# The end of a ranking: rows from a root, stores first, two groups in turns

## The chip, the cores and the metric

The kernel runs on one core of a Trainium2 chip. A core has five engines with queues of their own: TensorE (PE, with its weight load PEld), VectorE (DVE), ScalarE (ACT), GpSimd (POOL) and SyncE (SP), which here only issues transfers. Sixteen DMA engines move the data. The metric is device time of one execution in microseconds; smaller is better.

## The reference, cut to what matters

The program is a network of four layers on a tensor of 4 x 64 channels x 128 x 128, 12 ms long. The change lies in layer 1, in the first of its two parts. There each of 256 images (128 rows of 128 values each) gets a 128 x 128 matrix of squared distances between its rows, and every entry is replaced by a weight that depends only on its rank among all 16,384 entries of that image:

```python
def score_to_weight(score):
    n = shp[-1] * shp[-2]
    flat = score.reshape(-1, n)
    tau = jnp.argsort(-flat, axis=-1)
    ranks = (jnp.argsort(tau, axis=-1) + 1).astype(score.dtype) / n
    weights = -jnp.log(ranks).reshape(shp)
    return weights / jnp.sum(weights, axis=-1, keepdims=True)
```

The matrix is symmetric, so only the 8128 pairs above its diagonal are sorted. A pair's two entries take two ranks that follow each other. Where two distances are equal, the stable order of `argsort` decides, and that needs the places (row and column) of the pairs concerned.

## The kernel before, in words

**The ranking (`l1_ranks`).** The 256 images are two groups `g` of 128, one image to a partition. `keys[g]` is a tile of 128 x 8192 f32 (8128 pairs and padding). A merging network sorts it, and stores for each of its 91 stages which pairs turned (`sort_stage`, DVE, ACT and POOL). `number` marks equal neighbours in `ranks[g]`, an int16 tile of 128 x 8192. Then the stages are run backwards over the ranks (`back_stage`, DVE and ACT), so that each rank comes to stand at the place of its pair. The sorting and the way back take from 2004 to 5131 us of the profile.

**The end of the ranking (`finish`, L1548 to L1634),** called for group 0 and then for group 1. The steps that matter:

- *cast:* ACT copies the ranks to f32 into the group's own `keys` tile, free by then (L1551).
- *candidates:* DVE takes the eight largest of each of 32 segments of 256, with their indices (L1555, L1556). Marked ranks are above the others, so these are the pairs with equals.
- *spread:* DVE takes the marks off with an AND (L1558); ACT writes rank + 129 and rank + 130 beside each other as int16 into the tile `spare`, in two activations (L1561); SP stores the result to the memory tensor `pk[g]`, one transfer for each of the 127 rows of the matrix above the diagonal, since they shrink from 127 entries to one (L1565).
- *list:* the 64 largest candidates are found by eight rounds of MAX8 and MATCH_REPLACE8 (L1580, L1582), and their fields taken apart (L1586 to L1589): the pair's number `f`, whether it is equal to the next (`more`) and `tied`.
- *row:* `f` is compared with the 128 row ends, a constant tile loaded from memory, and the hits are summed (L1596, L1601); the column follows from the row (L1603 to L1607).
- *order among equals:* positions are compared all with all, 128 x 128 a partition, into the group's `keys` tile, and summed (L1620, L1625).
- *turn:* column, row and lack of each listed pair are copied to `both`, transposed on PE and copied to `ties` by ACT (L1631 to L1634).

`spare` is one tile for both groups. `cand`, `at`, `both` and the other small tiles have two buffers. Last, `m` collects a flag that says whether equals were too many for the list (L1656 to L1662); all engines load it, and an `If` (L1833) runs a slow full sort when it is set, which it is not here. Behind the `If` stands `l1_blocks`, which loads constants and then the stored ranks.

**What sets the order.** Sorting and the way back are in an order written out by hand. The end of the ranking is not: a scheduler orders the instructions of each engine at build time by their dependencies, so pieces of group 1 stand between those of group 0 already. Within an engine, instructions go in that order; SP issues its transfers one after the other.

Of the kernel before, what the change touches and what calls it, by code (L numbers as in the profile page):

```python
# [10 lines left out]
F32 = mybir.dt.float32  # L11
I32 = mybir.dt.int32
U32 = mybir.dt.uint32
I8, I16 = mybir.dt.int8, mybir.dt.int16
U8 = mybir.dt.uint8
BF16 = mybir.dt.bfloat16
AF = mybir.ActivationFunctionType
ALU = mybir.AluOpType
AX = mybir.AxisListType
# [3 lines left out]
P = 128  # L23
B, H, W, C = 4, 64, 128, 128
# [1025 lines left out]

def l1_constants():

    return {"l1c_rowend": np.asarray(ROW0[1:] + [1 << 20], np.float32),
            "l1c_diag": np.ascontiguousarray(np.diag(np.arange(1, W + 1)).reshape(W * W), np.int32)}


def rnn_inputs(env, x, xn, gram):
# [349 lines left out]
ROW0 = [n * (2 * W - 1 - n) // 2 for n in range(W)]  # L1407

SEG, TIES = 256, 64
# [43 lines left out]
def l1_ranks(env, dscr, keys, pk, masks, ties, tables):  # L1453
# [5 lines left out]
    nc, tc = env.nc, env.tc  # L1459
# [3 lines left out]
    with ExitStack() as ctx:  # L1463
        kp = ctx.enter_context(tc.tile_pool(name="sk", bufs=1))
        mp = ctx.enter_context(tc.tile_pool(name="sm", bufs=3))
        sb = ctx.enter_context(tc.tile_pool(name="sb", bufs=2))
        ranks = [kp.tile([P, NSORT], I16, name="rank%d" % g) for g in range(2)]
        bad = kp.tile([P, 2, 34], F32, name="bad")
        rowend = kp.tile([P, W], F32, name="rowend")
        nc.sync.dma_start(rowend, tables["rowend"].partition_broadcast(P))  # L1470
        segs = kp.tile([P, NSORT // SEG, 8], I32, name="segs")
        nc.gpsimd.iota(segs, [[SEG, NSORT // SEG], [0, 8]], base=0, channel_multiplier=0)
        place = kp.tile([P, 2 * TIES], I32, name="place")
# [5 lines left out]
        base = kp.tile([P, 2], F32, name="base")  # L1479
# [64 lines left out]

            nc.vector.tensor_scalar(bad[:, g, 0:1], v[:, 0:1], 1e-30, None, ALU.is_le)

        def finish(g, ta, tb):

            r = ranks[g]
            rf = ta  # L1550
            nc.scalar.copy(rf, r)  # L1551
            cand = sb.tile([P, NSORT // SEG, 8], F32, name="cand")
            at = sb.tile([P, NSORT // SEG, 8], U32, name="at")
            for s in range(NSORT // SEG):
                nc.vector.max(cand[:, s, :], rf[:, s * SEG : (s + 1) * SEG])  # L1555
                nc.vector.max_index(at[:, s, :], cand[:, s, :], rf[:, s * SEG : (s + 1) * SEG])  # L1556

            nc.vector.tensor_single_scalar(r, r, 16382, ALU.bitwise_and)  # L1558
            pt = tb.bitcast(I16).rearrange("q (f s) -> q f s", s=2)
            for s in range(2):  # L1560
                nc.scalar.activation(pt[:, :, s], r, AF.Identity, bias=base[:, s : s + 1])  # L1561
            pv = pk[g][0 : P * W * W, :].rearrange("(t f) o -> t (f o)", t=P)
            pi = tb.bitcast(I32)
            for n in range(W - 1):
                nc.sync.dma_start(  # L1565
                    pv[:, n * W + n + 1 : (n + 1) * W], pi[:, ROW0[n] : ROW0[n] + W - 1 - n]
                )

            nc.vector.tensor_scalar(bad[:, g, 1:33], cand[:, :, 7], 16383.5, None, ALU.is_gt)
            ci = sb.tile([P, NSORT // SEG, 8], I32, name="ci")  # L1570
            cp = sb.tile([P, NSORT // SEG, 8], I32, name="cp")
            nc.vector.tensor_tensor(ci, at.bitcast(I32), segs, ALU.add)
            nc.vector.tensor_copy(cp, cand)
            nc.vector.tensor_single_scalar(cp, cp, 13, ALU.logical_shift_left)
            nc.vector.tensor_tensor(cp, cp, ci, ALU.bitwise_or)
            nc.vector.tensor_single_scalar(cp, cp, 1 << 29, ALU.bitwise_or)
            cf = cp.rearrange("q s e -> q (s e)").bitcast(F32)
            top = sb.tile([P, TIES], F32, name="top")
            for t in range(0, TIES, 8):
                nc.vector.max(top[:, t : t + 8], cf)  # L1580
                if t + 8 < TIES:
                    nc.vector.match_replace(cf, top[:, t : t + 8], cf, 0.0)  # L1582

            def field(name, shift, mask):
                a = sb.tile([P, TIES], I32, name="fi")
                nc.vector.tensor_single_scalar(a, top.bitcast(I32), shift, ALU.logical_shift_right)  # L1586
                nc.vector.tensor_single_scalar(a, a, mask, ALU.bitwise_and)
                f = sb.tile([P, TIES], F32, name=name)
                nc.vector.tensor_copy(f, a)  # L1589
                return f  # L1590

            f, more, tied = field("f", 0, 8191), field("more", 13, 1), field("tied", 27, 1)
            nc.vector.tensor_copy(bad[:, g, 33:34], tied[:, TIES - 1 : TIES])

            cmp = ta.rearrange("q (i n) -> q i n", n=W)
            nc.vector.tensor_tensor(  # L1596
                cmp, f.unsqueeze(2).to_broadcast([P, TIES, W]), rowend.unsqueeze(1).to_broadcast([P, TIES, W]),
                ALU.is_ge,
            )
            row = sb.tile([P, TIES], F32, name="row")  # L1600
            nc.vector.tensor_reduce(row, cmp, AX.X, ALU.add)  # L1601
            col = sb.tile([P, TIES], F32, name="col")
            nc.vector.tensor_scalar(col, row, -0.5, W - 0.5, ALU.mult, ALU.add)  # L1603
            nc.vector.tensor_mul(col, col, row)
            nc.vector.tensor_sub(col, f, col)
            nc.vector.tensor_add(col, col, row)
            nc.vector.tensor_scalar(col, col, 1.0, None, ALU.add)  # L1607
            pos = sb.tile([P, 2, TIES], F32, name="pos")
            nc.vector.scalar_tensor_tensor(pos[:, 0, :], row, float(W), col, ALU.mult, ALU.add)
            nc.vector.scalar_tensor_tensor(pos[:, 1, :], col, float(W), row, ALU.mult, ALU.add)  # L1610

            run = sb.tile([P, TIES], F32, name="run")
            nc.vector.tensor_scalar(more, more, -1.0, 1.0, ALU.mult, ALU.add)
            nc.vector.tensor_tensor_scan(run, one, more, 0.0, ALU.mult, ALU.add)
            for s in range(2):
                nc.vector.scalar_tensor_tensor(pos[:, s, :], run, -32768.0, pos[:, s, :], ALU.mult, ALU.add)
            pf = pos.rearrange("q s i -> q (s i)")
            n2 = 2 * TIES
            before = ta.bitcast(I16).rearrange("q (i j) -> q i j", j=n2)
            nc.vector.tensor_tensor(  # L1620
                before, pf.unsqueeze(1).to_broadcast([P, n2, n2]), pf.unsqueeze(2).to_broadcast([P, n2, n2]), ALU.is_lt
            )
            rk = sb.tile([P, 2, TIES], F32, name="rk")
            rv = rk.rearrange("q s i -> q (s i)")
            nc.vector.tensor_reduce(rv, before, AX.X, ALU.add)  # L1625
            nc.vector.tensor_add(rv, rv, listed)
            nc.vector.tensor_mul(rk, rk, tied.unsqueeze(1).to_broadcast([P, 2, TIES]))
            for k, pair in enumerate(((col, row), (row, col), (rk[:, 0], rk[:, 1]))):
                both = sb.tile([P, 2, TIES], F32, name="both")
                for h in range(2):  # L1630
                    nc.vector.tensor_copy(both[:, h], pair[h])  # L1631
                pt = psum.tile([P, P], F32, name="pt")
                nc.tensor.transpose(pt, both.rearrange("q s i -> q (s i)"), env.ident)  # L1633
                nc.scalar.copy(ties[:, k, g * P : g * P + P], pt)  # L1634
# [4 lines left out]
        with tc.tile_pool(name="low", bufs=2, space=PSUM) as lows, tc.tile_pool(  # L1639
            name="diff", bufs=4  # L1640
# [4 lines left out]
        spare = ctx.enter_context(tc.tile_pool(name="spare", bufs=1)).tile([P, NSORT], F32, name="spare")  # L1645
        for g in range(2):
            number(g, keys[g], spare)
        with tc.manual_schedule(engines={E.Activation, E.DVE}):
            for i in range(ns):
                for g in range(2):  # L1650
                    back_stage(g, ns - 1 - i)
        psum = ctx.enter_context(tc.tile_pool(name="sp", bufs=1, space=PSUM))
        finish(0, keys[0], spare)
        finish(1, keys[1], spare)
        m = kp.tile([P, 1], F32, name="m")
        nc.vector.tensor_reduce(m, bad, AX.XY, ALU.max)  # L1656
        pm = psum.tile([1, P], F32, name="pm")
# [1728 lines left out]
def metaformer(tc, a, out, cst):  # L3386

    with ExitStack() as ctx:
        env = Env(ctx, tc)
        nc = tc.nc  # L3390
        dp = ctx.enter_context(tc.tile_pool(name="dram", bufs=1, space=DRAM))
        state = [dp.tile([NI, W, C], F32, name="state%d" % i) for i in range(5)]
        tokens = dp.tile([NI, W, C], F32, name="tokens")
        dist = dp.tile([NI, W * W], F32, name="dist")

        pk = [dp.tile([P * W * W, 1], I32, name="pk%d" % g) for g in range(2)]
        masks = [dp.tile([P, sum(NSORT // (2 * p) * (p - k if k < p else p) for p, k in merge_network(NSORT))], I8,
                         name="masks%d" % g) for g in range(2)]
        def part(prefix):
            return {k[len(prefix) :]: v for k, v in a.items() if k.startswith(prefix)}  # L3400

        x = a["x"].rearrange("b h w c -> (b h) w c")
        f0, f2 = part("L0_ffn_"), part("L2_ffn_")

        def diagonals():
# [5 lines left out]
        l0_conv(env, x, state[0], tokens, part("L0_conv_"), cst, diagonals)  # L3411
        rnn_ffn(env, state[0], state[1], f0["W"], f0["VT"], f0["gamma"], f0["beta"])
        l1_layer(
            env, state[1], state[2], dist, pk, masks, part("L1_conv_"), part("L1_ffn_"), {"rowend": cst["l1c_rowend"]}
        )
        l2_conv(env, state[2], state[3], part("L2_conv_"))
        rnn_ffn(env, state[3], state[4], f2["W"], f2["VT"], f2["gamma"], f2["beta"])
# [37 lines left out]
```

## Time and profile before

| | us |
|---|---|
| median of 3 runs | 11948.84 |
| lowest, highest of them | 11933.74, 11949.3 |
| the profiled execution | 11937.16 |
| its span | 11935.4 |
| distances and all before, 0 to 2003.7 | 2003.7 |
| sorting and way back, to 5123.4 | 3119.7 |
| end of the ranking, 5123.4 to 5325.3 | 201.9 |
| layer 1's blocks, to 6300 | 974.7 |
| the rest | 5635 |

Over the whole span DVE is busy 84%, ACT 63%, PE 61%, POOL 52%. These shares mix stages with different limits: in the end of the ranking DVE is busy 184.2 of 201.9 us, ACT 53.0, PE 3.1 and POOL 0.2. A line of the profile's order of time gives start, length, engine, line of the kernel, operation, the tiles written and read, shapes and count, and in brackets how long the engine had been idle and what ended that. A name such as SPq is the engine's queue, in which transfers are issued.

### The profile page before, as it was taken

What the parts mean: (1) busy time and instruction counts of PE and PEld (TensorE: products, weight loads), DVE (VectorE), ACT (ScalarE), POOL (GpSimd) and SP (SyncE); (2) the same over time, 40 slices, a digit from 0 to 9 for tenths busy, and PEclk for the clock granted to TensorE, in tenths of its full rate; (3) what the DMA queues carried; (4) which work ended last, traced back from release to release, by engine and by line L of the source; (5) the groups of instructions that cost most, each with busy time, mean ns of one, the idle gap of its engine ahead of it and who ended that gap; (6) DMA issues with size and microseconds to landing.
All of it is one profiled execution on the core that took longest, in us unless ns stands there. A gap on an engine that the chain in (4) does not pass through costs nothing. (4 is left out here: it accounts for less than half of the span.)

```text
span 11935.4 us, 113939 instructions
## 1 busy us (share of the span) xinstructions
PE 7337.1 (61%) x33966; PEld 4454.9 (37%) x33966; DVE 10014.6 (84%) x16358; ACT 7522.4 (63%) x10863; POOL 6182.3 (52%) x5276
## 2 busy tenths in 40 slices
PE   7887796000000000009998899989999999998665
PEld 5665564000000000008886344444444444446443
DVE  7566637999999999988996899999999999996444
ACT  4255534888867777633332778777878787875332
POOL 1000016999970000002332899998999999994222
PEclk8876798555555555559999899999999999999887
DMA  4223245111111111121111343433333334333434
GB/s 139 89 43 100 63 149 140 56 57 58 58 56 54 55 54 56 49 49 42 47 45 35 129 143 140 144 135 137 135 140 139 143 138 143 139 133 117 169 131 152
DMA packets 632396, 1193.48 MB, mean 100 GB/s; under 512 B 216556, under 2 KB 433998, under 8 KB 552398
## 3 DMA queue, kind: packets, MB, share of 16 engines
q1 hardware_dynamic: 587550, 1043.02, 26.1%
q0 software_dynamic: 34656, 140.92, 3.6%
q8 instruction: 274, 4.49, 0.2%
q10 hardware_dynamic: 9552, 2.08, 0.1%
q14 instruction: 364, 2.98, 0.1%
HBM read 950.89 MB, written 251.71 MB: 101 GB/s over the span
## 5 line engine op out<-in xcount | busy, mean ns | idle before, releaser
L2717 POOL TENSOR_TENSOR gs<-hist,cc 128x512 f32<-128x512 f32 x2048 | 2576.5, 1266 | 378.9 <-DVE hist L2712 217.1
L2712 DVE TENSOR_TENSOR_SCAN hist<-da,state,bs 128x512 f32<-128x512 f32 x1984 | 2523.9, 1272 | 0.0
L2726 PE MATMUL py<-gs,ident 128*128 128x512 f32 x4096 | 2246.0, 631 | 5.1 <-DVE y L2602 3.7
L1633 PE MATMUL pt<-ident,both 128*128 128x128 f32 x6 | 2.7, 447 | 3258.0 <-DVE both L1631 3258.0
L2683 ACT ACTIVATE da<-dt,am 128x512 f32<-128x512 f32 x2048 | 1414.8, 715 | 325.6 <-DVE hist L2712 323.0
L2704 DVE TENSOR_TENSOR bs<-dx,bs 128x512 f32<-128x512 f32 x2048 | 1393.8, 681 | 187.7 <-PE bs L2690 143.0
L1509 POOL TENSOR_TENSOR diff<-key 128x2048 f32<-128x2048 f32 (+11 forms) x364 | 1383.8, 3861 | 86.8 <-DVE key L1514 75.2
L1633 PEld LDWEIGHTS pt<-ident,both 128*128 128x128 f32 x6 | 1.1, 183 | 3259.5 <-issue 3259.5
L2726 PEld LDWEIGHTS py<-gs,ident 128*128 128x128 f32 x4096 | 739.3, 197 | 902.5 <-issue 441.2
L1884 POOL IOTA row<- 72x1 int32 x1 | 0.1, 136 | 1800.7 <-ACTq L1833 1800.7
L2690 PE MATMUL bs<-bt,pick 96*128 96x512 bf16 x2048 | 807.3, 394 | 140.3 <-DVE hist L2712 137.3
L1531 ACT COPY keep<-rank 128x1536 int16<-128x1536 int16 (+11 forms) x364 | 612.8, 1686 | 437.9 <-DVE rank L1533 389.0
L1507 ACT COPY low<-key 128x2048 f32<-128x2048 f32 (+11 forms) x364 | 626.7, 1722 | 285.1 <-DVE key L1514 276.4
L1532 DVE COPY_PREDICATED rank<-back,rank 128x1536 int16<-128x1536 uint8 (+11 forms) x364 | 781.8, 2148 | 16.7 <-ACT keep L1531 16.7
L1533 DVE COPY_PREDICATED rank<-back,keep 128x1536 int16<-128x1536 uint8 (+11 forms) x364 | 778.0, 2137 | 12.5
L1514 DVE TENSOR_TENSOR key<-low,key 128x2048 f32<-128x2048 f32 (+11 forms) x364 | 744.5, 2045 | 12.4
L1513 DVE TENSOR_TENSOR key<-low,key 128x2048 f32<-128x2048 f32 (+11 forms) x364 | 749.2, 2058 | 6.5 <-DMA key<-dist 6.2
L1510 ACT ACTIVATE turned<-diff 128x2048 int8<-128x2048 f32 (+11 forms) x364 | 600.0, 1697 | 36.4 <-DMA key<-dist 27.6
L1522 ACT ACTIVATE back<-turned 128x3072 uint8<-128x3072 int8 (+12 forms) x182 | 582.3, 3200 | 0.0
L2183 PE MATMUL pe<-ew,xg 128*128 128x128 f32 x4096 | 504.4, 277 | 0.0
L1031 POOL DMA_DIRECT2D state<-zz x16 | 18.6, 1161 | 909.7 <-DVE zz L1021 854.5
L2183 PEld LDWEIGHTS pe<-ew,xg 128*128 128x128 f32 x4096 | 488.2, 193 | 3.9
(826 smaller groups left out, 18502.8 us busy)
## 6 DMA issues: line engine op xcount, KB each, us to landing
cc<-cd SPq DMA_DIRECT2D x512, 1024.0 KB
xt<-state SPq DMA_DIRECT2D x64, 1024.0 KB
xo<-state SPq DMA_DIRECT2D x128, 256.0 KB
state<-xo POOLq DMA_DIRECT2D x128, 256.0 KB, 2.8
xl<-in_L_ffn_weight SPq DMA_DIRECT2D x32, 1024.0 KB
tk<-in_x SPq DMA_DIRECT2D x32, 512.0 KB
tokens<-tt POOLq DMA_DIRECT2D x32, 512.0 KB, 5.2
tk<-tokens SPq DMA_DIRECT2D x8, 2048.0 KB
```

The costliest lines, as they stand in the source:

```text
L1509: nc.gpsimd.tensor_sub(d, lo[part], hi[part])
L1513: nc.vector.tensor_tensor(lo[part], c, hi[part], ALU.min)
L1514: nc.vector.tensor_tensor(hi[part], c, hi[part], ALU.max)
L1532: nc.vector.copy_predicated(l, t, h)
L1533: nc.vector.copy_predicated(h, t, kv)
L2183: T.matmul(w["pe"][:, j, :], w["xg"][:, q, j, :], ew[:, q, :], start=False, stop=(j == 3 and q == E - 1))
L2683: nc.scalar.activation(da, x_["dt%d" % b], AF.Exp, scale=am[:, s : s + 1])
L2690: nc.tensor.matmul(bs, pick[:, s, :], x_["bt%d" % b], start=True, stop=True)
L2704: nc.vector.tensor_mul(db, x_["dx%d" % b], db)
L2712: nc.vector.tensor_tensor_scan(h, live.pop(("da", t)), live.pop(("db", t)), 0.0 if first else state[b][:, s : s + 1], ALU.mult, ALU.add,)
L2717: nc.gpsimd.tensor_tensor(gs, h, live.pop(("cc", t)), ALU.mult)
L2726: nc.tensor.matmul(x_["py%d" % b], env.ident, live.pop(("gs", t)), start=(s == 0), stop=(s == S - 1))
```

## The change

`finish` is cut into `spread`, `candidates`, `equals`, `compare` and `lacking`, and these are called for the two groups in turns. Group 1's ranks are spread into `keys[1]` in place of `spare`, and group 1's comparison of all with all goes into `keys[0]`. The AND and the stores are put ahead of the candidates. The row of a listed pair is no longer found with 128 comparisons: it is the rounded value of a root, (255 - sqrt(255^2 - 8 f)) / 2, the root made by Ln and Exp on ACT, and is then put right by one down or up by looking whether `f` lies before the row's start or behind its end. The constant of row ends is gone, with its load.

```diff
-        rowend = kp.tile([P, W], F32, name="rowend")
-        nc.sync.dma_start(rowend, tables["rowend"].partition_broadcast(P))
...
-        def finish(g, ta, tb):
+        def spread(g, pt):
             r = ranks[g]
-            rf = ta
-            nc.scalar.copy(rf, r)
...
+            nc.vector.tensor_single_scalar(r, r, 16382, ALU.bitwise_and)
+            halves = pt.bitcast(I16).rearrange("q (f s) -> q f s", s=2)
+            for s in range(2):
+                nc.scalar.activation(halves[:, :, s], r, AF.Identity, bias=base[:, s : s + 1])
+            pv = pk[g][0 : P * W * W, :].rearrange("(t f) o -> t (f o)", t=P)
+            pi = pt.bitcast(I32)
+            for n in range(W - 1):
+                nc.sync.dma_start(
+                    pv[:, n * W + n + 1 : (n + 1) * W], pi[:, ROW0[n] : ROW0[n] + W - 1 - n]
+                )
+
+        def candidates(g, rf):
             cand = sb.tile([P, NSORT // SEG, 8], F32, name="cand")
...
+            return cand, at
+
+        def equals(g, cand, at):
...
-            cmp = ta.rearrange("q (i n) -> q i n", n=W)
-            nc.vector.tensor_tensor(
-                cmp, f.unsqueeze(2).to_broadcast([P, TIES, W]), rowend.unsqueeze(1).to_broadcast([P, TIES, W]),
-                ALU.is_ge,
-            )
+            x = sb.tile([P, TIES], F32, name="x")
+            nc.vector.tensor_scalar(x, f, -8.0, float((2 * W - 1) ** 2), ALU.mult, ALU.add)
+            nc.vector.tensor_scalar(x, x, 1.0, None, ALU.max)
+            nc.scalar.activation(x, x, AF.Ln)
+            nc.scalar.activation(x, x, AF.Exp, scale=0.5)
+            ri = sb.tile([P, TIES], I32, name="ri")
+            nc.vector.tensor_scalar(ri, x, -0.5, W - 0.5, ALU.mult, ALU.add)
             row = sb.tile([P, TIES], F32, name="row")
-            nc.vector.tensor_reduce(row, cmp, AX.X, ALU.add)
+            nc.vector.tensor_copy(row, ri)
+            gap = sb.tile([P, TIES], F32, name="gap")
+
+            def start():
+                nc.vector.tensor_scalar(gap, row, -0.5, W - 0.5, ALU.mult, ALU.add)
+                nc.vector.tensor_mul(gap, gap, row)
+                nc.vector.tensor_sub(gap, f, gap)
+
+            start()
+            nc.vector.scalar_tensor_tensor(row, gap, 0.0, row, ALU.is_lt, ALU.subtract)
+            nc.vector.tensor_scalar(row, row, -1.0, None, ALU.mult)
+            start()
+            nc.vector.tensor_add(x, gap, row)
+            nc.vector.scalar_tensor_tensor(row, x, W - 1.0, row, ALU.is_ge, ALU.add)
+            start()
             col = sb.tile([P, TIES], F32, name="col")
-            nc.vector.tensor_scalar(col, row, -0.5, W - 0.5, ALU.mult, ALU.add)
-            nc.vector.tensor_mul(col, col, row)
-            nc.vector.tensor_sub(col, f, col)
-            nc.vector.tensor_add(col, col, row)
-            nc.vector.tensor_scalar(col, col, 1.0, None, ALU.add)
+            nc.vector.scalar_tensor_tensor(col, gap, 1.0, row, ALU.add, ALU.add)
...
-        finish(0, keys[0], spare)
-        finish(1, keys[1], spare)
+        for g in range(2):
+            nc.scalar.copy(keys[g], ranks[g])
+        spread(0, spare)
+        found = [candidates(0, keys[0])]
+        found.append(candidates(1, keys[1]))
+        last = [equals(0, *found[0])]
+        before = [compare(last[0][3], keys[0])]
+        spread(1, keys[1])
+        last.append(equals(1, *found[1]))
+        lacking(0, *last[0][:3], before[0])
+        before.append(compare(last[1][3], keys[0]))
+        lacking(1, *last[1][:3], before[1])
```

`compare` holds the comparison of all with all (L1620 before), and `lacking` its sum and the turn to `ties` (L1625 to L1634).

More of the change, by code (lines that the diff above doesn't have):

```diff
@@ L1051, in l1_constants @@
 def l1_constants():
-    return {"l1c_rowend": np.asarray(ROW0[1:] + [1 << 20], np.float32),
-            "l1c_diag": np.ascontiguousarray(np.diag(np.arange(1, W + 1)).reshape(W * W), np.int32)}
+    return {"l1c_diag": np.ascontiguousarray(np.diag(np.arange(1, W + 1)).reshape(W * W), np.int32)}
 def rnn_inputs(env, x, xn, gram):
@@ L1556, in finish @@
                 nc.vector.max_index(at[:, s, :], cand[:, s, :], rf[:, s * SEG : (s + 1) * SEG])
[L1558 to L1566, printed above, removed]
-                )
+            return cand, at
+        def equals(g, cand, at):
             nc.vector.tensor_scalar(bad[:, g, 1:33], cand[:, :, 7], 16383.5, None, ALU.is_gt)
@@ L1593, in finish @@
             nc.vector.tensor_copy(bad[:, g, 33:34], tied[:, TIES - 1 : TIES])
-            cmp = ta.rearrange("q (i n) -> q i n", n=W)
-            nc.vector.tensor_tensor(
-                cmp, f.unsqueeze(2).to_broadcast([P, TIES, W]), rowend.unsqueeze(1).to_broadcast([P, TIES, W]),
-                ALU.is_ge,
-            )
-            row = sb.tile([P, TIES], F32, name="row")
-            nc.vector.tensor_reduce(row, cmp, AX.X, ALU.add)
-            col = sb.tile([P, TIES], F32, name="col")
-            nc.vector.tensor_scalar(col, row, -0.5, W - 0.5, ALU.mult, ALU.add)
-            nc.vector.tensor_mul(col, col, row)
-            nc.vector.tensor_sub(col, f, col)
-            nc.vector.tensor_add(col, col, row)
-            nc.vector.tensor_scalar(col, col, 1.0, None, ALU.add)
+            x = sb.tile([P, TIES], F32, name="x")
[5 more added lines that the diff above has]
+            nc.vector.tensor_scalar(ri, x, -0.5, W - 0.5, ALU.mult, ALU.add)
+            row = sb.tile([P, TIES], F32, name="row")
+            nc.vector.tensor_copy(row, ri)
[11 more added lines that the diff above has]
+            start()
+            col = sb.tile([P, TIES], F32, name="col")
+            nc.vector.scalar_tensor_tensor(col, gap, 1.0, row, ALU.add, ALU.add)
             pos = sb.tile([P, 2, TIES], F32, name="pos")
@@ L1616, in finish, with compare @@
                 nc.vector.scalar_tensor_tensor(pos[:, s, :], run, -32768.0, pos[:, s, :], ALU.mult, ALU.add)
+            return row, col, tied, pos
+        n2 = 2 * TIES
+        def compare(pos, room):
             pf = pos.rearrange("q s i -> q (s i)")
-            n2 = 2 * TIES
-            before = ta.bitcast(I16).rearrange("q (i j) -> q i j", j=n2)
+            before = room.bitcast(I16).rearrange("q (i j) -> q i j", j=n2)
             nc.vector.tensor_tensor(
@@ L1622, in finish, with lacking @@
             )
+            return before
+        def lacking(g, row, col, tied, before):
             rk = sb.tile([P, 2, TIES], F32, name="rk")
@@ L3413, in metaformer @@
         l1_layer(
-            env, state[1], state[2], dist, pk, masks, part("L1_conv_"), part("L1_ffn_"), {"rowend": cst["l1c_rowend"]}
+            env, state[1], state[2], dist, pk, masks, part("L1_conv_"), part("L1_ffn_"), {}
         )
```

## The prediction, made before the changed kernel ran

> **What bounds the kernel now.** I began with the busy time of each engine in stretches of the span, to find the changed part and see who works there. Columns: stretch, its length, then busy time and instruction count of PE, PE's weight load, DVE, ACT, POOL.
>
> ```profile
> 5123.40:5175.10 51.70, 0.00 (x0) 0.00 (x0) 51.63 (x170) 32.74 (x5) 0.00 (x0) 0.50 0.00 0
> 5175.10:5235.50 60.40, 1.34 (x3) 0.55 (x3) 60.40 (x67) 0.80 (x3) 0.00 (x0) 0.50 0.31 69
> 5235.50:5262.00 26.50, 0.00 (x0) 0.00 (x0) 25.84 (x64) 18.70 (x2) 0.00 (x0) 0.50 0.01 0
> 5262.00:5324.10 62.10, 1.72 (x4) 0.63 (x4) 46.30 (x27) 0.80 (x3) 0.14 (x1) 0.50 0.31 68
> ```
>
> The end of the ranking takes 201 us of 11935.4. DVE is full for three stretches, but in the last it works 46.3 of 62.1 us: something else ends the stage. The transfers run in the second and fourth stretch only (31% of the DMA engines), so I asked for the stores of the ranks and for the order of time around them (start, length, engine, line, operation, count).
>
> ```profile
> L1565 SPq DMA_DIRECT2D pk<-spare x254: 319/430/1406, 5175.1 to 5323.3; - x127
> ```
> ```profile
> 5123.42 7.01 ACT L1551 CAST key<-rank 128x8192 f32<-128x8192 int16 x1
> ...
> 5131.15 7.02 ACT L1551 CAST key<-rank 128x8192 f32<-128x8192 int16 x1 [0.72 <-DVE rank L1533]
> ...
> 5154.06 2.28 DVE L1558 TENSOR_SCALAR rank<-rank 128x8192 int16<-128x8192 int16 x1
> ...
> 5156.37 18.69 ACT L1561 ACTIVATE spare<-rank,base 128x8192 int16<-128x8192 int16 x2 [18.20 <-DVE rank L1558]
> ...
> 5171.62 8.68 DVE L1596 TENSOR_TENSOR key<-f,rowend 128x8192 f32<-128x8192 f32 x1
> ```
> ```profile
> 5192.59 17.22 DVE L1620 TENSOR_TENSOR key<-pos 128x16384 int16<-128x16384 f32 x1
> ...
> 5243.28 18.70 ACT L1561 ACTIVATE spare<-rank,base 128x8192 int16<-128x8192 int16 x2 [13.30 <-DVE rank L1558]
> ...
> 5309.17 0.27 ACT L1634 COPY ties<-pt 128x128 f32<-128x128 f32 x1 [17.93 <-PE pt L1633]
> ```
> ```profile
> 5325.28 0.17 DVE L1868 MEMSET rw<- 128x128 f32 x1 [16.73 <-SPq L1833]
> 5325.37 0.39 SPq L1847 DMA_DIRECT2D enc<-in_L_conv_enc_w  x1
> ```
>
> SP issues 127 stores a group. Group 0's run from 5175.1 to 5235.5 (60.4 us, 0.476 each), group 1's from 5262.0 to 5323.7 (61.7 us); between them SP stands 26.5 us, because both groups go through the one tile `spare`, which ACT fills for group 1 only at 5243.3 to 5262.0. DVE and ACT are done at 5309.4; then DVE waits 16.7 us for SP at the `If` (L1833). So **SP's stores set the end of this stage**, and everything after it starts at 5325.3.
>
> **What the Trainium skill says.** *Perfetto Trace Analysis*, What "DMA-bound" means: a kernel can be bound by the issuing sequencer, its track solid with DMA slices, which are descriptor generation and not data movement. The trace agrees: issues back to back at 0.476 us with DMA engines 31% busy. *ScalarE: Activation LUTs*, Table sets: Ln and Exp share one set, so that the pair needs one load. Here Ln and Exp of L1950 and L1951 run at 5348.73 and 5348.97 with no load ahead since the distances, and in the changed kernel's order no load stands ahead of the new pair. *ScalarE*, What ACT_TABLE_LOAD costs: an activation takes 186 ns + 0.833 ns an element, an estimate of 0.24 us for 64; the trace has 0.26 us for 128x64 (L2126).
>
> **The change part by part.** The built order of instructions gives each engine's sequence; I walk it with the trace's durations.
>
> *Ranks first (ACT, SP).* The AND on group 0's ranks goes ahead of the 32 pairs of maximum and index search (5131.01 to 5154.06, 23.05 us), so it runs from 5131.0 to 5133.2, off ACT's path. ACT does both casts first (the second ends at 5138.2), then the two spreading activations: 5138.2 + 18.7 = 5156.9. SP starts there and not at 5175.1: **18.2 us earlier**. Group 0's stores end at 5156.95 + 60.4 = 5217.4.
>
> *Second buffer.* Group 1's spread goes into `keys[1]`, free once group 1's candidates have been read. DVE: 5133.2 + 2 x 23.05 = 5179.3, three small operations (0.1 + 0.33 + 0.2), AND 2.2: 5182.2. ACT: 5182.25 + 18.7 = 5200.9, which is 16.5 us before SP needs it. So SP's gap of **26.5 us goes**; the wait of this activation on all the earlier stores goes as well, since it has no DMA wait in the new order. SP: 5217.4 + 61.7 = 5279.1, last issue and branch 0.4: 5279.5. Before it branched at 5324.1: 44.6 earlier. If the cover of 16.5 us failed, each us beyond it would be paid.
>
> *Root in place of the table (DVE).* Out: per group one 8.68 us compare (L1596) and one 8.68 us sum (L1601), issued 8.6 apart: 4 x 8.6 = 34.4 us. In: 13 more operations of 128x64 a group (18 in place of 5); the trace gives 0.10 to 0.12 us each where another group's stand between, 0.2 us alone. 26 x 0.12 = 3.1 us. On ACT, Ln and Exp twice; they are queued behind group 1's spread, which the new order makes ACT finish at 5200.9, then two of 0.26 in a chain: DVE can go on at 5201.5.
>
> *DVE's walk.* At 5182.2: rest of the key building of both groups 2.0 us, 16 MAX8 at 0.33 and 14 replace pairs at 0.39 = 10.7, fields, scan and the two operations ahead of Ln 3.1: 5198.0. Wait for ACT to 5201.5 (3.5 us). Then 39 small operations at 0.12 to 0.13: 5206.5. Then compare 17.14 (issue to issue), four small 0.6, sum 17.12, a few small 0.4, compare 17.14, 0.2, sum 17.12: 5276.2. A check by difference: before, DVE took 5131.0 to 5308.5 = 177.5; less 34.4, plus 3.1, plus 3.5, less about 3 us of latency gaps that group 1's lone chain had (5243 to 5253 and 5271 to 5273) and that turns now fill: 146.7, so 5277.7.
>
> *Tail.* Both `both` buffers are full, so four transposes with their ACT copies (0.45 + 0.27 + semaphores, about 0.78 each) and the last operations of group 1 come after the last sum: ACT ends near 5280.0. Before, one stood there. Then the branch: ACT's came 0.4 us after its copy (5309.8) and its first semaphore event after it at 5313.1. These 3.3 us were hidden under SP's stores; **now they are late next**: 5280.0 + 0.4 + 3.3 = 5283.7, while SP is through at 5279.5 + 1.3 = 5280.8. SP's first load after the `If` waits on ACT and DVE, so it goes at about 5283.7 and not at 5325.37: **gain 41.7 us**.
>
> *At nothing.* The `rowend` load leaves SP's queue at 2044.4, where SP is idle till its next issue at 2047.5 for lack of masks; if it were not hidden, 0.33 us gained. Three more 256-byte tiles move addresses only. PE now transposes `m` first; `m` is ready at about 5198, before any `both`.
>
> Sum: 11937.16 (profiled execution; its span 11935.4) - 41.7 = 11895.5. The median shown is 11948.84 over 11933.74 to 11949.3; from it, 11907.1. I take the middle, **11902**.
>
> **Bounds on what the trace does not show.** The branch's 3.3 us exposed: from nothing (SP last, gain 44.6) to 3.3. Small operations in turns: 0.10 to 0.2 us over 39 + 26, so DVE from 1.5 us less to 5 us more. Ln and Exp: no load in the order; were there one it is 1.28 us by the row at 5349.19. Store rate beside other DVE work: 0.476 to 0.486 in both stretches, so 0 to 2.5 us. Together a gain of 34 to 45 us.
>
> **Rivals.**
> 1. *Only the earlier start is won.* Something still holds group 1's spread until group 0's stores have landed, and SP's gap stays 20 us or more: 5217.4 + 26.5 + 61.7 leaves 18.2 us, 11919 to 11931. For: SP still runs both groups in order. Against: the tiles differ, and the activation waits on DVE and ACT alone. 4%.
> 2. *DVE becomes the clear bound.* ACT's spread slows or the root's chain runs at 0.3 us a step: DVE ends 8 to 14 us later, gain 27 to 34, 11908 to 11918. For: after the change DVE and SP end within 3 us of each other, so any slip shows in full. Against: the steps have the other group's between them. 12%.
> 3. *SP stays last* with the branches hidden: gain 44.6, 11892 to 11904. 20%.
> 4. *Slower.* The stores now overlap DVE's candidate search and ACT's spread; if this stretched each from 0.476 us, SP, which has 254 in one line, would take the whole loss. It decides at 44.6 / 254 = 0.176 us more, 0.65 a store; at 0.75 the time would be 11968. For: a single store took up to 1.4 us. Against: the second stretch, with ACT idle, and the first have the same 0.43 us median. 3%.
> 5. *It does not do what it says*: a compiler that keeps one order for both groups, so nothing is gained, 11940. The built order excludes most of it. 1%.
>
> **How the numbers follow.** The forecast has 60%: gain 36 to 44, 11890 to 11914 over the two baselines. With rivals 2 and 3 the gain runs from 27 to 45; taken against a baseline that itself moves over 15 us, eight in ten lie in 11887 to 11918. About 0.2% (24 us) is what a measurement of this kernel can tell from no change. Faster by more: the forecast, rivals 2 and 3 (92%), less some 3% for a baseline drawn low: 0.89. Within: rivals 1 and 5 and that 3%: 0.08. Slower: 0.03.
>
> **What would show it.** Stores of group 0 begin near 5157 and SP has no gap near the 128th; ACT's third spread begins near 5182 with a wait on DVE; the two 8.68 us rows are gone; DVE waits about 3.5 us for ACT's Exp; the first load after the `If` comes near 5284, released by ACT's or DVE's branch and not by SP's. A gap in SP, a table load, or stores over 0.5 us apart would show me wrong.

## The result, and the profile after

| | before | after |
|---|---|---|
| median of 5 runs, us | 11948.84 | 11889.27 |
| lowest to highest, us | 11932.91 to 11949.59 | 11866.29 to 11901.57 |
| profiled execution, its span, us | 11937.16, 11935.4 | 11866.29, 11864.5 |

The ratio is 0.9954, 95% interval 0.9941 to 0.9968: faster by 0.46%, some 55 us, and by more than 0.2% over the whole interval. The prediction said 11902 in a range of 11887 to 11918.

Times within the profiles do not compare directly, since the stages ahead of the change, which it leaves alone, ended 4.7 us later in this execution. From here on *the stage* runs from the end of the way back on DVE (the AND's start after the change, the first search for candidates before it) to the first load behind the `If`. Before, it ran from 5131.0 to 5325.4, **194.4 us**; after, from 5135.7 to 5288.2, **152.5 us**. That is 41.9 us less, where the prediction had 41.7.

The busy time of the engines in stretches of the span, after the change, cut at the first store, between the groups and at the branch (stretch, length, then PE, PE's weight load, DVE, ACT, POOL, each with its count, then TensorE's granted clock, the busy share of the DMA engines and GB/s):

```profile
5135.70:5161.50 25.80, 0.00 (x0) 0.00 (x0) 25.80 (x100) 25.59 (x3) 0.00 (x0) 0.50 0.00 0
5161.50:5222.10 60.60, 0.37 (x1) 0.08 (x1) 57.59 (x221) 19.22 (x6) 0.00 (x0) 0.50 0.31 69
5222.10:5283.00 60.90, 1.95 (x5) 0.81 (x5) 60.24 (x23) 1.06 (x4) 0.00 (x0) 0.50 0.31 69
5283.00:5288.20 5.20, 0.88 (x2) 0.29 (x2) 0.00 (x0) 0.53 (x2) 0.01 (x1) 0.50 0.04 6
```

Of before's four stretches the third, 26.5 us with no store, is gone, and the first, ahead of the stores, is 25.8 us from the stage's start where it was 44.1. DVE is now busy through both stretches of stores but for one wait of 2.9 us, where it stood for 16 us in the second. A new stretch has come at the end: 5.2 us in which nothing but a few transposes and copies of 0.3 us runs.

The stores, from the view of their line after the change (shortest, median, longest issue in ns, first and last start):

```profile
L1554 SPq DMA_DIRECT2D pk<-spare x127: 319/430/558, 5161.5 to 5221.6; - x127
L1554 SPq DMA_DIRECT2D pk<-key x127: 320/430/485, 5222.2 to 5282.1; - x127
```

And in order of time (start, length, engine, line, operation; in brackets the idle time ahead and its end):

```profile
5142.79 18.66 ACT L1550 ACTIVATE spare<-rank,base 128x8192 int16<-128x8192 int16 x2
...
5187.01 18.69 ACT L1550 ACTIVATE key<-rank,base 128x8192 int16<-128x8192 int16 x2 [25.56 <-DVE rank L1547]
...
5206.12 0.34 DVE L1602 TENSOR_SCALAR ri<-x 128x64 int32<-128x64 f32 x2 [2.94 <-ACT x L1600]
...
5211.08 17.22 DVE L1639 TENSOR_TENSOR key<-pos 128x16384 int16<-128x16384 f32 x1
...
5263.73 17.21 DVE L1648 TENSOR_REDUCE rk<-key 128x128 f32<-128x16384 int16 x1
```
```profile
5284.27 0.27 ACT L1657 COPY ties<-pt 128x128 f32<-128x128 f32 x1 [0.57 <-PE pt L1656]
5288.19 0.40 SPq L1880 DMA_DIRECT2D enc<-in_L_conv_enc_w  x1
5288.19 0.14 POOL L1917 IOTA row<- 72x1 int32 x1 [1770.89 <-ACTq L1866]
5288.27 0.17 DVE L1901 MEMSET rw<- 128x128 f32 x1 [5.36 <-ACTq L1866]
```

Group 1's spread now waits for DVE's AND alone and is done 16 us ahead of the first store that needs it. Behind the `If`, DVE waits for ACT's queue (ACTq), where it had waited 16.7 us for SP's. The view of the `If`'s line says what lies between ACT's last copy and there:

```profile
L1866 SPq COMPARE_BRANCH  x1: 50/50/50, 5283.0 to 5283.0; - x1
...
L1866 ACTq COMPARE_BRANCH  x1: 45/45/45, 5284.9 to 5284.9; - x1
...
L1866 ACTq EVENT_SEMAPHORE  x1: 17/17/17, 5288.1 to 5288.1; - x1
```

SP is at its branch at 5283.0. ACT branches at 5284.9 and shows its next event at 5288.1: 3.2 us that stand on the path now. Before, the same stretch on ACT ended 11 us ahead of SP's branch:

```profile
L1833 ACTq COMPARE_BRANCH  x1: 45/45/45, 5309.8 to 5309.8; - x1
...
L1833 ACTq EVENT_SEMAPHORE  x1: 17/17/17, 5313.1 to 5313.1; - x1
L1833 SPq COMPARE_BRANCH  x1: 50/50/50, 5324.1 to 5324.1; - x1
```

### The profile page after: what moved, and what is told of

It is laid out like the page before. It is cut to its first block, busy times and chain, and to the rows that moved or that the text cites. A ratio compares the mean times of both kernels' runs of the same rounds, so it can differ in the third digit from the quotient of the medians.

```text
span 11864.5 us, 114000 instructions
## 1 busy us (share of the span) xinstructions
PE 7305.2 (62%) x33966; PEld 4440.4 (37%) x33966; DVE 9976.4 (84%) x16380; ACT 7521.5 (63%) x10867; POOL 6181.0 (52%) x5276
## 5 line engine op out<-in xcount | busy, mean ns | idle before, releaser
L1529 DVE COPY_PREDICATED rank<-back,rank 128x1536 int16<-128x1536 uint8 (+11 forms) x364 | 781.7, 2147 | 16.7 <-ACT keep L1528 16.7
```

The costliest lines, as they stand in the source:

```text
L1529: nc.vector.copy_predicated(l, t, h)
```

## Experiments

All are compared by the length of the stage in their profile and by their time against the kernel before, run beside them. The kernel before had a median of 11915.91 us beside the first four and of 11925.71 beside the last three, in later sessions than the first measurement; so ratios are compared, and not times across sessions.

### One buffer for both groups

```diff
-        spread(1, keys[1])
+        spread(1, spare)
```

> The changed kernel with group 1's ranks spread into spare again, so one buffer for both groups; nothing else. Stage means: from the end of the way back on DVE to the first load behind the If; it was 194.4 us before and 152.5 after the change. In the built order Ln and Exp now stand ahead of group 1's spread, and the spread waits for all stores. Theory (the tile shared by the groups made SP's gap): SP starts as in the changed kernel, ends group 0's stores 86 us into the stage, the spread runs from 88 to 107, stores to 168, stage 169 us, 16 to 17 us longer than after the change; DVE ends near 145 and waits for SP. Rival (order alone made the gain, the gap had another cause): stage 152 to 154. Rival (all the gain is DVE's): 150 to 153.

Measured: stage **171.2 us**; ratio 0.9986 (0.9978 to 0.9995). In order of time:

```profile
5189.89 0.26 ACT L1600 ACTIVATE x<-x 128x64 f32<-128x64 f32 x1
5212.05 0.27 ACT L1657 COPY ties<-pt 128x128 f32<-128x128 f32 x1 [21.90 <-PE pt L1656]
5212.35 18.71 ACT L1550 ACTIVATE spare<-rank,base 128x8192 int16<-128x8192 int16 x2
...
5293.76 0.17 DVE L1901 MEMSET rw<- 128x128 f32 x1 [27.79 <-SPq L1866]
5293.82 0.39 SPq L1880 DMA_DIRECT2D enc<-in_L_conv_enc_w  x1
```

The stage starts at 5122.6 here. The last Exp of the root is done at 5190.2, group 0's last store is issued at 87.0 us into the stage (5209.6), and the spread starts at 89.7. SP stands from 87.0 to 108.4, and its stores end at 169.4 instead of 146.9. So a shared tile alone, in the new order, costs 18.7 us of the stage. Against before this kernel still gains 23.2: 18.3 by the earlier start of the ranks, and the rest because SP stands 21.4 us between the groups and not 26.5. The stage is 2 us longer than expected: the built order had put ACT's first copy of `ties` ahead of the spread, and SP's last issue to the first load took 1.8 us. Both rivals fall, that the order alone made the gain and that all of it is DVE's.

### The table in place of the root

The constant of row ends and its load come back too. The table needs the room of `keys[0]`, so group 1's list now comes after group 0's sum; what is measured is the table together with this order.

```diff
+            cmp = ta.rearrange("q (i n) -> q i n", n=W)
+            nc.vector.tensor_tensor(cmp, f.unsqueeze(2).to_broadcast([P, TIES, W]),
+                rowend.unsqueeze(1).to_broadcast([P, TIES, W]), ALU.is_ge)
             row = sb.tile([P, TIES], F32, name="row")
+            nc.vector.tensor_reduce(row, cmp, AX.X, ALU.add)
...
-        last.append(equals(1, *found[1]))
         lacking(0, *last[0][:3], before[0])
+        last.append(equals(1, *found[1], keys[0]))
```

> The changed kernel with the row of a listed pair found by the table of 128 row ends again, the table's comparison for both groups in keys[0], so group 1's after group 0's sum. Theory (after the change DVE ends last and the join's branch is exposed): SP ends 148 us into the stage as after the change, DVE pays 4 x 8.6 = 34.4 us more, less 3 for the root's small operations, less 2.9 for the wait on ACT, and about 2 for group 1's lone chain: stage 181 us, plus or minus 3, so 13 us less than before and 28 more than after. Rival (SP's stores alone set the end): stage 150 to 154, as after the change.

Measured: stage **178.6 us**; ratio 0.9986 (0.9977 to 0.9995). SP's stores end at 147.6 us into the stage, as after the change; the end is DVE's and ACT's:

```profile
L1557 SPq DMA_DIRECT2D pk<-key x127: 320/430/440, 5220.1 to 5280.1; - x127
```
```profile
5289.77 17.22 DVE L1638 TENSOR_REDUCE rk<-key 128x128 f32<-128x16384 int16 x1
...
5290.47 0.27 ACT L1647 COPY ties<-pt 128x128 f32<-128x128 f32 x1 [17.07 <-PE pt L1646]
...
5308.67 0.27 ACT L1647 COPY ties<-pt 128x128 f32<-128x128 f32 x1 [17.93 <-PE pt L1646]
5311.60 0.39 SPq L1870 DMA_DIRECT2D enc<-in_L_conv_enc_w  x1
```

The last sum ends, ACT copies, and 2.7 us after ACT the first load goes. The root, with the turns that it allows, is worth 26.1 us once the stores are out of the way. That is 2 us less than expected, and the difference lies behind the last sum: here ACT's last copy ends 2.0 us after it and the first load goes 2.7 us later, where after the change it was 3.6 and 3.65. The rival that SP's stores alone set the end after the change falls.

### The root alone

```diff
         (the kernel before)
-            cmp = ta.rearrange("q (i n) -> q i n", n=W)
...
-            nc.vector.tensor_reduce(row, cmp, AX.X, ALU.add)
+            nc.scalar.activation(x, x, AF.Ln)
+            nc.scalar.activation(x, x, AF.Exp, scale=0.5)
...
+            nc.vector.scalar_tensor_tensor(row, x, W - 1.0, row, ALU.is_ge, ALU.add)
```

> The kernel before with the root in place of the table and nothing else moved. Theory (SP's stores set the end before the change, and group 1's spread lets them start): DVE is 28 us shorter, but in the built order group 1's Ln and Exp stand ahead of its spread on ACT, so the spread starts near 111 us into the stage, where it was 112.3; stores end near 192, stage 193 us against 194.4: a gain of 0 to 4 us. Rival (DVE, busy 84% of the span and 184 of 202 us of this stage, is the bound): stage 166 us, a gain of 28.

Measured: stage **192.2 us**; ratio 1.0006 (0.9997 to 1.0015). In order of time:

```profile
5241.26 0.26 ACT L1595 ACTIVATE x<-x 128x64 f32<-128x64 f32 x1 [19.36 <-DVE x L1594]
5241.54 0.26 ACT L1596 ACTIVATE x<-x 128x64 f32<-128x64 f32 x1
5241.84 18.71 ACT L1558 ACTIVATE spare<-rank,base 128x8192 int16<-128x8192 int16 x2
...
5282.80 0.27 ACT L1644 COPY ties<-pt 128x128 f32<-128x128 f32 x1 [17.93 <-PE pt L1643]
```
```profile
5323.63 0.17 DVE L1878 MEMSET rw<- 128x128 f32 x1 [41.46 <-SPq L1843]
```

The constant of row ends and its load are gone here too. ACT's last copy comes at 151.6 us into the stage where it came at 178.4 before: DVE and ACT did get 26.8 us shorter. The spread of group 1 starts 1.9 us earlier only (110.4 against 112.3), for it stands on ACT behind Ln and Exp of its own group. So the stage gains 2.2 us, DVE waits 41.5 us for SP where it waited 16.7, and the total does not move by anything that can be measured. The root is worth 26.1 us with the stores early and 2.2 without. The rival that DVE is the bound, with a gain of 28 us, falls.

### Without the `If`

```diff
-        flag = nc.values_load(mi[0:1, 0:1], min_val=0, max_val=1, ...)
-        with tc.If(flag > 0):
-            l1_sort(env, dscr, pk, ties)
```

> The changed kernel without the load of the flag and the If; the slow full sort for too many equals is left out, which these inputs do not take. Theory (3.3 to 3.6 us between ACT's last copy and the first load behind the If are the branch on ACT): the first load comes 147.5 to 149.5 us into the stage and not at 152.5, 3 to 5 us earlier. Rival (the wait is for landed stores or for something else in the join): 152 to 153.

Measured: first load **148.6 us** into the stage; ratio 0.9969 (0.9955 to 0.9983).

```profile
5269.07 0.48 PE L1656 MATMUL pt<-ident,both 128*128 128x128 f32 x1 [0.35 <-ACT ties L1657]
5269.58 1.36 SPq L1910 DMA_DIRECT2D left<-in_L_ffn_expert_b  x4
5269.59 0.27 ACT L1657 COPY ties<-pt 128x128 f32<-128x128 f32 x1 [0.57 <-PE pt L1656]
```

The first load follows the end of PE's last transpose (5269.55) directly, 3.9 us earlier in the stage than with the `If`. It is another load than before, since the scheduler now puts four pieces of `left` ahead of `enc`, which goes at 150.1, 2.4 us earlier than with the `If`. So the stretch between ACT's last copy and the first load belongs to the flag's load and the branch, which went together, and the prediction had read the branch from ACT's events; what takes the time in it is not shown.

### A part of the stores from POOL

```diff
-                nc.sync.dma_start(
+                (nc.gpsimd if n % 7 in (2, 5) else nc.sync).dma_start(
```

> The changed kernel with two of seven row stores issued by POOL in place of SP (72 of 254). From the rows of the kernel before, a store takes SP 0.476 us and POOL 1.2 us: both queues are done near 113 us into the stage, 34 us before they were. Theory (after the change DVE's sums, ACT's last copies and the branch end the stage; SP's stores end 2 us before ACT and no longer count): stage 152.5 us as after the change, within 1 us. Rival (SP's stores still set the end): stage 149 or less, or shorter in step with SP. If POOL's issues slow DVE, the stage gets longer by as much.

Measured: stage **152.5 us**; ratio 0.9970 (0.9959 to 0.9981). The stores by line:

```profile
L1554 SPq DMA_DIRECT2D pk<-key x91: 319/430/455, 5198.7 to 5241.8; - x91
...
L1554 POOL DMA_DIRECT2D pk<-key x36: 541/541/546, 5198.9 to 5217.6; - x36
```
```profile
5281.26 0.17 DVE L1901 MEMSET rw<- 128x128 f32 x1 [5.24 <-ACTq L1866]
```

SP ends at 113.6 us into the stage, 33 us earlier than before this edit, and the stage stays as it was to a tenth of a us. After the change the stores no longer set the end, though they come within 2 us of it. The expectation had POOL's price wrong: 0.54 us a store and not 1.2. It had taken the row of POOL's stores of 1024 KB (`dist<-o`); those of 256 KB (`state<-xo`) took 0.54 us in the same profile.

### Shorter sums on top

```diff
-            before = room.bitcast(I16).rearrange("q (i j) -> q i j", j=n2)
+            before = room.bitcast(BF16).rearrange("q (i j) -> q i j", j=n2)
...
-            nc.vector.tensor_reduce(rv, before, AX.X, ALU.add)
+            for h in (64, 32, 16):
+                nc.vector.tensor_add(before[:, :, 0:h], before[:, :, 0:h], before[:, :, h : 2 * h])
+            nc.vector.tensor_reduce(rv, before[:, :, 0:16], AX.X, ALU.add)
```

> The kernel of the split stores, and each sum of the 128 x 128 comparisons (17.1 us) made by three pairwise additions in bf16 of 8192, 4096 and 2048 results and a sum over the last 16 of each row; the comparison writes bf16 in place of int16, and counts up to 128 are exact in it. If the additions run at two elements a cycle as an estimate from the rate of 16384 in 17.1 us, they take 4.3, 2.1 and 1.1 us and the last sum 2.2 us: 9.8 us, 7.3 less for each group. Theory (DVE ends last): ACT's last copy comes near 134 us into the stage, stage 137 to 140 us, 13 to 15 less than after the change. Rival (at one element a cycle): 17 us again, stage 152 to 153. Rival (stores bind): 152.

Measured: stage **137.3 us**; ratio 0.9948 (0.9934 to 0.9962). The additions by line:

```profile
L1649 DVE TENSOR_TENSOR key<-key x6: 1219/2285/4420, 5214.4 to 5249.4; 128x8192 bf16<-128x8192 bf16 x2, 128x4096 bf16<-128x4096 bf16 x2, 128x2048 bf16<-128x2048 bf16 x2
```

At the end the first load goes, and DVE waits as before for ACT's queue:

```profile
5258.55 0.39 SPq L1882 DMA_DIRECT2D enc<-in_L_conv_enc_w  x1
...
5258.62 0.17 DVE L1903 MEMSET rw<- 128x128 f32 x1 [4.58 <-ACTq L1868]
```

With the stores off the path, what DVE saves comes through: 4.42 + 2.29 + 1.22 and a last sum of 2.28 us, 10.2 in place of 17.2, are some 14 us for two groups. The stage lost 15.2, as ACT's last copy also ends 2.0 us after the last sum and not 3.6, with more of the transposes made ahead of it. In the stage this version beats both kernels. Its total beat the kernel before; beside the changed kernel (11862.88 against 11870.46 us median) the intervals overlap, and more runs would be needed to tell them apart in the total.

### The changed kernel again

No edit; the same kernel beside the last two.

> The changed kernel itself, beside the others on the same chip. Theory (the change gains what the stage lost, 42 us, and the rest of the 55 us measured first was the scatter of the 6600 us behind the stage, which ran 33 us apart in the two profiles): ratio near 0.9965, within 0.995 to 0.998. Rival (some 13 us more are gained behind the stage): 0.9954 or less.

Measured: stage **152.4 us**; ratio 0.9955 (0.9942 to 0.9969).

This does not settle between the two by itself: the interval holds 0.9965, and the middle is at the rival's figure. What the other runs add is in this table. The time behind the stage is code that the change does not touch. The clock is TensorE's granted clock, the mean over the profiled execution; the last column is explained below.

| kernel | stage saved, us | total saved by the ratio, us (interval) | behind the stage in the profile, us | clock of the profile | total saved at equal clock, us (standard error) |
|---|---|---|---|---|---|
| before | | | 6610.0 | 0.788 | |
| changed, first time | 41.9 | 55 (38 to 70) | 6576.3 | 0.791 | |
| changed, again | 42.0 | 54 (37 to 69) | 6611.2 | 0.788 | 43 (4) |
| part of the stores from POOL | 41.9 | 36 (23 to 49) | 6624.5 | 0.788 | 37 (3) |
| one buffer | 23.2 | 17 (6 to 26) | 6590.4 | 0.790 | 22 (2) |
| table | 15.8 | 17 (6 to 27) | 6607.2 | 0.788 | 16 (2) |
| root alone | 2.2 | -7 (-18 to 4) | 6604.9 | 0.788 | 1 (2) |
| no `If` (to the first load) | 45.8 | 37 (20 to 54) | | 0.791 | 41 (3) |
| shorter sums | 57.1 | 62 (45 to 79) | 6592.5 | 0.791 | 57 (4) |

The stage's saving lies within every interval. The three measurements with a stage of 152.5 us save 55, 54 and 36 us in total, and the same kernel ran 6576.3 and 6611.2 us behind the stage in its two profiles. That is a scatter of single executions larger than the disputed 13 us.

The scatter goes with the clock. The three profiles at 0.790 or 0.791 ran 6576.3 to 6592.5 us behind the stage, the five at 0.788 ran 6604.9 to 6624.5. Over the 108 executions of this section, each with its clock on record, a straight-line fit (one slope, and a level for each kernel and each set of runs of the kernel before) gives 9.8 us less for 0.001 more. A shorter stage lifts the mean clock by itself, since the clock is 0.50 in the stage: 42 us less of it lift the mean by about 0.001, an estimate from 42 x (0.789 - 0.50) / 11,870. With this share left to the kernel, the fit gives the last column. It lies within 6 us of the stage's saving in every row, and the changed kernel gains 43 us, with a standard error of 4. So the runs of this section give no sign of 13 us gained behind the stage; that its first measurement drew high clocks is likely, but cannot be reckoned the same way, since the clocks of the runs of the kernel before, but for the profiled one, are not on record there.

## Why the prediction was right

*SP's stores set the end before.* Held, and the root alone shows it most sharply: 26.8 us came off the time at which DVE and ACT were done, 2.2 off the stage.

*Ranks first, 18.2 us earlier.* Into the stage, SP started at 44.1 before and at 25.8 after: 18.3.

*Second buffer, gap of 26.5 us gone.* The first store of group 1 follows the last of group 0 at once, at the same 0.476 us a store. The cover was put at 16.5 us: the spread ended at 5205.7 and was needed at 5222.2. The reason given, the one tile for both groups, is only part of it. In the prediction's own line of before, group 1's spread (5243.28) was released by DVE's AND, 7.8 us after the last store's issue at 5235.5, and not by the stores. So by this reading a second tile in the old order would have left the gap as it was; it needed the AND put earlier as well. With the order and one tile 21.4 us of the gap stay. The second tile alone was not run.

*DVE's walk.* No table load stood between the distances, where the last one began at 1804.7, and Ln and Exp at 5205.56. That agrees with the Trainium skill (*ScalarE: Activation LUTs*, Table sets), by which the two share one set. DVE waited 2.9 us for Exp (3.5 predicted), began the first comparison 75.4 us into the stage (75.5) and the last sum ended at 145.2 (145.2, with starts put at 5131.0). ACT's last copy ended at 148.8 (149.0).

*The branch is late next.* 3.65 us from ACT's last copy to the first load (3.7), and taking the `If` away gave 3.9 us back. Of the rivals, the one with SP last is refused by the stores from POOL, and the one with DVE far behind by DVE's walk, which met its times; the slower one by the unchanged rate of the stores beside the search for candidates.

*The total.* The forecast of 11902 us stands 13 us over the median of 11889.27. This lies 2 us inside the wide range and just below the 11890 to 11914 of the forecast itself, so that the total fell inside was in part luck; what held is the stage, whose sum missed by 0.2 us. The rest is the baseline and the untouched 6600 us. The prediction gave them some 15 us of room, and the 6600 us moved by 48 us between profiles of kernels that end the stage at the same time, with the granted clock, which the prediction left out. Two of its ranges do not follow exactly from its sums: a gain of 36 to 44 off 11937 and 11949 is 11893 to 11913, and 27 to 34 (the second rival) is 11903 to 11922.

## What to carry to other kernels

Before shortening the busiest engine of a stage, look who is waited for at its end: here DVE was busy 184.2 of 201.9 us, and taking 27 us from it changed next to nothing until SP's transfers could start and run without a gap. Here the many small stores on one queue were two stretches of 60 to 62 us in every order tried with SP alone, so it paid to move their start and fill their gap first. Ask for every cause of such a gap: here it was the tile, and an instruction that came late on another engine. Then the other chain is worth shortening, and what the old bound had covered, like a branch, comes out.

## What the runs showed of the hardware

- Behind the `If`, whose long body is skipped, ACT showed nothing for 2.5 to 3.3 us and DVE for 2.9 to 3.1 us after the branch, SP only for 0.2 us, over the eight traces that have it. What takes the time is not shown.
- A store of up to 500 bytes in each of 128 partitions kept POOL 0.54 us and landed 1.7 to 3.3 us after; SP took 0.476 us from one to the next for stores of up to 508 bytes. POOL's stores of 1024 KB ahead of the sort had taken 1.2 us.
- An addition of two bf16 tiles of 8192 results took 4.42 us, where DVE's sum over 16384 int16, another operation, took 17.21: 1850 results a us against 950 elements.
